# Planning layer 0's first expert block into the routing stage of a two-layer adaLN kernel

## The chip, the cores and the metric

The kernel runs on one core of a Trainium2 chip. The metric is device time in microseconds (us), the median of several runs. Engines: PE (TensorE, matrix multiply), DVE (VectorE), ACT (ScalarE), POOL (GpSimd, which here issues the indirect DMAs, that is, gathers and scatters by an index) and SP (SyncE, which issues plain DMAs).

## What is computed

Two layers on `x` of 4 x 1024 tokens with 256 features, everything in 32-bit floats. Each layer modulates normalised rows by a conditioning vector, adds a gated attention-like term, and then a gated mixture of experts. The change concerns layer 0's experts:

```python
h = _layernorm(x, axis=-1) * (1 + cb) + sb
x = x + gb * _L0_ffn_ref(h, ...)

# _L0_ffn_ref
logits = jnp.einsum('bsd,de->bse', input_emb, Wr) + br
route_w = jax.nn.softmax(logits, axis=-1)
_, topk_idx = jax.lax.top_k(route_w, TOP_K)          # 2 of 8 experts
...
h = jax.nn.relu(jnp.einsum('bsd,edh->ebsh', input_emb, W1) + b1[:, None, None, :])
expert_out = jnp.einsum('ebsh,ehd->ebsd', h, W2) + b2[:, None, None, :]
return jnp.einsum('bse,ebsd->bsd', routed, expert_out)
```

An expert maps 256 features to 1024 hidden units (W1) and back to 256 (W2).

## The kernel before

**Stage one** (to about 114 us) computes layer 0's attention term and the routing. Its work is a list of pieces given to a small planner, the class `Plan`: each piece has an engine, an estimated duration, the pieces it must follow, the buffers it holds, and a rank (lower goes first). `plan.run()` simulates the engines with these estimates and then emits the pieces in the order of their simulated start; on PE, ACT, DVE and POOL the instructions stand in exactly that order, and each engine executes its own list in order. The kernel's own estimates thus only set an order. SP's pieces are DMAs.

Normalised rows are stored into the DRAM table `h_rows` (one row of 256 features and two numbers, the "marks" `g_meta`, for each token), 512 KB at a time (L1318), and the marks by a second small DMA (L1305).

**Grouping tokens by expert.** Every token-expert pair is put into blocks of 128 pairs that share an expert. With counts of pairs by expert (`turn`, `total_staged`, `bases`), `close_staged` (a chain of small DVE operations, L598 to L651) works out which block belongs to which expert, `across` (PE, L690) spreads this over the partitions, `limits` (DVE) makes the limits of each block, and `list_weights` (DVE) the indices by which a block's weights are gathered. For one block j, `reach` (DVE, L754, tile `g_reached`), `look` (PE, L767, `pm_counts`) and `find` (DVE, L780 and L789) give the row numbers of its 128 tokens; `fetch` (POOL, L349, `xg`) gathers these rows. Block 0 is special: its limits come from `begin` alone, without `close_staged`. At the end of stage one, blocks 0, 1 and 2 are looked up. `kept_busy` puts matmuls of no use to the result on PE (`pm_busy`, L917).

**Stage two** runs the blocks in a loop written out by hand. Block j: transpose the gathered rows (`turn_rows`, PE, L1682, `pm_x`), copy them out of PSUM (`rows_turned`, DVE, L1687, `xT`), `hidden` (PE, L1729, `p_h`, 16 matmuls in two groups of eight), `rectified` (ACT, L1741, `hid`, bias and ReLU), `values` (PE, L1752, `p_y`, eight matmuls), `biased` (DVE, `y`), and a scatter of the result (POOL). In iteration j stand, in this order on PE: hidden(j), the transposes of block j+1, look-ups of later blocks, values(j-1). Weights lie in two buffers each for W1 and W2; `weights_in(j+1)` gathers W1 for the next block and does nothing where the expert is the one that the buffer already holds. The buffers of blocks 0 and 1 are loaded early in stage one by `first_weights` (SP), together with the gate `gb0` (128 x 1024 floats), which is first used after all of layer 0's early blocks.

The order around the change comes from the planner in stage one and from the loop in stage two. PSUM is shared out by three pools (`ps_1` and `ps_m` with three buffers, `ps_2` with two), handed out in turn: a piece that takes a buffer waits for the last reader of the one before it.

Of the kernel before, what the change touches and what calls it, by code (L numbers as in the profile page):

```python
# [19 lines left out]
P = 128  # L20
# [3 lines left out]
E = 8  # L24
# [117 lines left out]
def adaln_d2_kernel(  # L142
# [218 lines left out]
    class Pairs:  # L361
# [225 lines left out]
        def close_staged(self, scratch):  # L587


            J, blocks, runs, origin, up1 = self.J, self.blocks, self.runs, self.origin, self.up1  # L590
            begin2 = float(J - LATE)

# [10 lines left out]
            nc.vector.tensor_copy(blocks[:, :, 1:], blocks_i)  # L603
# [304 lines left out]

    plan = Plan(p1=3, p2=2, pm=3, xn1=5, h1T=2, xn2=6, h2T=2, t1=1, le=2)
# [301 lines left out]
    def second_half(b):  # L1211
# [73 lines left out]
        for gs in routed:  # L1285
            k, at = 4 * len(gs), 4 * gs[0] * B + b
            tag = (b, gs[0])

            def route(k=k, at=at, tag=tag):
                g0.route(pa, tiles["pl", tag[0], tag[1]][:, :, :E], br_sb, at, k, B)  # L1290

            d = plan(
                DVE,
                0.24 * 14 + 0.16 * 4 if k == NC else 0.22 * 14,
                route,
                after=[ready[g][0] for g in gs],
                holds=[ready[gs[-1]][1]],
                rank=rank - 0.2,
            )
            for g in gs:  # L1300
                of_batch["route", b, g] = d

            def mark(k=k, at=at):
                first = at - at % B
                nc.sync.dma_start(  # L1305
                    h_rows[first * P : (first + k * B) * P, D:].rearrange(
                        "(c b p) d -> b p c d", b=B, p=P
                    )[at % B],
                    g0.meta[:, at : at + (k - 1) * B + 1 : B, :],
                )  # L1310

            plan("SP", 1.0, mark, after=[d], rank=rank)
            for g in gs:
                back, slot, key = backs[g]

                def store(g=g, key=key):
                    at = 4 * g * B * P
                    nc.sync.dma_start(  # L1318
                        h_rows[at : at + 4 * B * P, :D].rearrange(
                            "(c b p) d -> b p c d", b=B, p=P  # L1320
                        )[b],
                        tiles["xn", key],
                    )

                plan("SP", 4.0, store, after=back, holds=[slot], rank=rank)
# [18 lines left out]
    def first_weights():  # L1344

        for i in range(2):
            nc.sync.dma_start(w1buf[i], W1[(E - 1) * P :, :])
            nc.sync.dma_start(w2buf[i], W2[(E - 1) * P :, :])
        gate_in(1, gb0)
# [26 lines left out]
    for piece in range(3):  # L1376
        ps = plan.slot("p2")
        m = loaded
        for k in range(KD):

            def mm(piece=piece, k=k):
                if k == 0:
                    tiles["rows1", piece] = psum(ps_2, [B, 2 * D], "pm_mod")
                nc.tensor.matmul(
                    tiles["rows1", piece],
                    lhsT=sT1[:, k, :B],
                    rhs=tiles["wm1"][:, k, 2 * D * piece : 2 * D * (piece + 1)],
                    start=(k == 0),
                    stop=(k == KD - 1),
                )  # L1390

            m = plan(PE, 0.87, mm, after=[m, of_batch["routed"]], holds=[ps], rank=20.0)

        def out_(piece=piece):
            modulation1(tiles["rows1", piece], piece)

        plan(ACT, 0.8, out_, after=[m], holds=[ps], rank=20.0)
# [9 lines left out]
    d = plan(DVE, 3.9, lambda: g0.close_staged(pa), after=[m], holds=[ps], rank=-1.0)  # L1407
# [9 lines left out]
    ps = plan.slot("p1")  # L1417
    m = plan(PE, 0.4, lambda: g0.across(ps_1), after=[d], holds=[ps], rank=-1.0)
    kept_busy(1.1, [m], 30.0)
    d = plan(DVE, 1.4, lambda: g0.limits(pa), after=[m, bs], holds=[ps], rank=-1.0)  # L1420
    plan(DVE, 1.2, lambda: g0.list_weights(pa), after=[d], holds=[ps], rank=-0.75)
    for j in range(AHEAD):
        ps = plan.slot("p1")
# [10 lines left out]
        first = -1.0 + 0.1 * j if j else -1.6  # L1434
        r = plan(DVE, 0.5, reach, after=[d] if j else [begun], rank=first)
        m = plan(PE, 0.25, look, after=[r], holds=[ps], rank=first)
        plan(DVE, 0.6, find, after=[m], holds=[ps], rank=first if j else -0.95)
        if j < AHEAD - 1:
            kept_busy(0.7, [m], 30.0 + j)
# [239 lines left out]
    def turn_rows(j):  # L1679
        pt = psum(ps_m, [P, KD, P], "pm_x")  # L1680
        for k in range(KD):
            nc.tensor.transpose(pt[:, k, :], xgbuf[j % 4][:, k:D:KD], ident)  # L1682
        return pt

    def rows_turned(pt):
        xT = work.tile([P, KD, P], F32, tag="xT", name="xT", bufs=3)
        nc.vector.tensor_copy(xT, pt)  # L1687
        return [xT[:, k, :] for k in range(KD)]

    def in_quads(j):  # L1690
        return 3 * QUAD <= j < turning

    def rows_of_block(j):
        if in_quads(j):
            return xgquad[j // QUAD % 2][:, j % QUAD, :]
        return xgbuf[j % 4]

    def quad_turned(j):

        rows = xgquad[j // QUAD % 2]  # L1700
        square = quads.tile([P, P // SQ, KD, QUAD, SQ], F32, tag="square", name="square", bufs=1)
        for k in range(KD):
            nc.vector.transpose(
                square[:, :, k, :, :].rearrange("p m b s -> p b m s"),
                rows[:, :, k:D:KD].rearrange("p b (m f) -> p b m f", f=SQ),
            )
        xT = quads.tile([P, P // SQ, KD, QUAD, SQ], F32, tag="xTq", name="xTq")
        for q in range(P // SQ):
            for m in range(P // SQ):
                nc.sync.dma_start(  # L1710
                    xT[m * SQ : (m + 1) * SQ, q, :, :, :], square[q * SQ : (q + 1) * SQ, m, :, :, :]
                )
        for b in range(QUAD):
            turned_quads[j + b] = [xT[:, :, k, b, :] for k in range(KD)]
            dests[j + b] = g0.aim(work, rows[:, b, :], j + b)

    def weights_in(j):
        gather(w1buf[j % 2], W1, g0.wrow[:, j : j + 1], E * P - 1)

    def weights_out(j):  # L1720
        gather(w2buf[j % 2], W2, g0.wrow[:, j : j + 1], E * P - 1)

    def hidden(j, xT, m4):
        w1 = w1buf[j % 2]
        p1 = psum(ps_1, [P, 4, P], "p1_h")
        for i in range(4):
            m = 4 * m4 + i
            for k in range(KD):
                nc.tensor.matmul(  # L1729
                    p1[:, i, :],  # L1730
                    lhsT=w1[:, k * H + m * P : k * H + (m + 1) * P],
                    rhs=xT[k],
                    start=(k == 0),
                    stop=(k == KD - 1),
                )
        return p1

    def rectified(j, hid, p1, m4):
        for i in range(4):
            m = 4 * m4 + i  # L1740
            nc.scalar.activation(  # L1741
                hid[:, m, :],
                p1[:, i, :],
                AF.Relu,
                bias=w1buf[j % 2][:, KD * H + m : KD * H + m + 1],
            )

    def values(j, hid):
        w2 = w2buf[j % 2]
        p2 = psum(ps_2, [P, D], "p2_y")  # L1750
        for m in range(KH):
            nc.tensor.matmul(  # L1752
                p2,
                lhsT=hid[:, m, :],
                rhs=w2[:, m * D : (m + 1) * D],
                start=(m == 0),
                stop=(m == KH - 1),
            )
        return p2

    def biased(j, p2):
        y = work.tile([P, D], F32, tag="y", name="y", bufs=3)
        nc.vector.tensor_tensor(y, p2, w2buf[j % 2][:, KH * D :], ALU.add)  # L1763
        return y

    dests, ys0, turned_quads = {}, {}, {}

    def aimed(j):
        dests[j] = g0.aim(work, xgbuf[j % 4], j)

    def kept(j):
        put("g0", dests[j], ys0[j])

    def new_hidden():
        return work.tile([P, KH, P], F32, tag="hid", name="hid")


# [18 lines left out]
    def once(j):  # L1796

        if j in (4, 5):
            gate_of(rows1[:, 3 * j - 10, :], rows1[:, 3 * j - 10, :], work)
        if j == 5:  # L1800
# [6 lines left out]
    with tc.manual_schedule(engines=ORDERED | {EngineType.SP}):  # L1807
        looks = {0: (3,), 1: (4,)} | {j: (j + 3, j + 10) for j in range(2, 9)}
        fetches = {j: (j + 2,) for j in range(4)} | {j: (j + 2, j + 8) for j in range(4, 10)}
        for j in range(2):  # L1810
            g0.fetch(rows_of_block(j), h_rows, j)
        xT, hid = rows_turned(turn_rows(0)), None
        aimed(0)
        for j in range(turning):
# [11 lines left out]
            new = new_hidden()  # L1826
            for m4 in range(2):
# [9 lines left out]
            if j:  # L1837
                ys0[j - 1] = biased(j - 1, values(j - 1, hid))
            if j % QUAD == 0 and in_quads(j + QUAD):
# [773 lines left out]
```

## Time and profile before

| what | us |
|---|---|
| median of 5 runs | 1112.48 (1110.62 to 1114.46) |
| the profiled execution's own time | 1113.93 |
| its span, first to last instruction | 1112.2 |
| PE busy | 1068.5 |
| DVE, ACT, POOL busy | 588.2, 429.4, 423.0 |

The span is cut into 40 equal slices of 27.8 us in the page; the change lies in the fourth and fifth (83 to 139 us). A line of the timeline has start, duration, engine, source line, operation, tile written `<-` tile read, and in square brackets the time the engine sat idle before it and what ended that. The chain of waits is the sequence of work that ended last, followed back from the end. In a table of windows, "PEclk" is the clock that TensorE was granted, 1.00 being full speed.

### The profile page before, as it was taken

The numbers are of one execution on the slowest core, as the hardware profiler recorded it, in microseconds if no ns is written. First come the engines' busy times: TensorE is split into PE (matmuls) and PEld (weight loads), VectorE is DVE, ScalarE is ACT, GpSimd is POOL, SyncE is SP. The second block draws the span as 40 slices with busy tenths as digits, with TensorE's granted clock in tenths as the row PEclk, the third lists the DMA queues.
The fourth block names the chain that finished last, engine by engine and source line by source line (L and its number), as shares of the span: only waits on it lengthen the run. The fifth ranks groups of instructions, "written<-read, shape, count | busy, mean of one in ns | idle before, by whom it ended". The sixth has DMA issues, their size and how long they took to land.

```text
span 1112.2 us, 18513 instructions
## 1 busy us (share of the span) xinstructions
PE 1068.5 (96%) x6142; PEld 837.4 (75%) x6142; DVE 588.2 (53%) x2284; ACT 429.4 (39%) x1164; POOL 423.0 (38%) x483
## 2 busy tenths in 40 slices
PE   7998999999999999999999999999999999999994
PEld 5895899998999999999989465665666577656751
DVE  7787343222222222221156488878588535698657
ACT  5977233322323233333344333423325325442531
POOL 2000566554555555554454010110116322743745
PEclk8999999999999999999999999999999999999998
DMA  9404423666552625343071211210004322441544
GB/s 317 187 21 115 155 89 111 246 202 206 166 177 57 211 59 170 103 139 123 20 256 40 73 57 48 62 34 19 1 25 137 96 72 81 128 131 60 170 113 149
DMA packets 86910, 128.69 MB, mean 116 GB/s; under 512 B 30412, under 2 KB 66517, under 8 KB 82206
## 3 DMA queue, kind: packets, MB, share of 16 engines
q0 software_dynamic: 31872, 69.68, 20.3%
q1 hardware_dynamic: 53838, 56.22, 15.9%
q10 hardware_dynamic: 1104, 1.58, 0.4%
q8 instruction: 51, 0.84, 0.3%
q14 instruction: 45, 0.37, 0.1%
HBM read 205.25 MB, written 30.22 MB: 212 GB/s over the span
## 4 chain that ended last, share of the span: by engine, by line
PE 80%; DVE 8%; DMA 7%; ACT 3%; issue 2%; POOL 0%; SPq 0%; DVEq 0%; ACTq 0%; POOLq 0%
PE p_h L1729 20%; PE p_u L2052 19%; PE p_y L1752 19%; PE p_f L2100 10%; PE p_e L2360 4%; DMA w<-in_W,g_wrow 3%; PE pm_x L2343 1%; PE pm_t L1664 1%; DMA xg<-gb_rows,gb_row 1%; ACT xn L1004 1%; PE pm_counts L767 1%; DVE ln_st L978 1%; PE pm_gram L1130 1%; PE pm_b L1071 1%; DMA yg<-y 1%
## 5 line engine op out<-in xcount | busy, mean ns | idle before, releaser
L1741 ACT ACTIVATE hid<-p_h,w 128x128 f32<-128x128 f32 x544 | 154.9, 368 | 317.2 <-issue 238.0
L1752 PE MATMUL p_y<-w,hid 128*128 128x256 f32 x1088 | 250.1, 383 | 3.2 <-DMA w<-in_W,g_wrow 3.2
L2052 PE MATMUL p_u<-hT,a 128*128 128x512 f32 x512 | 231.6, 596 | 1.6 <-ACTq L2015 0.8
L1752 PEld LDWEIGHTS p_y<-w,hid 128*128 128x128 f32 x1088 | 202.6, 191 | 28.6 <-DMA w<-in_W,g_wrow 3.6
L1729 PEld LDWEIGHTS p_h<-xTq,w 128*128 128x128 f32 x1536 | 179.1, 192 | 2.5
L1729 PE MATMUL p_h<-xTq,w 128*128 128x128 f32 x1536 | 179.2, 275 | 0.0
L2052 PEld LDWEIGHTS p_u<-hT,a 128*128 128x128 f32 x512 | 93.7, 190 | 98.3 <-issue 89.5
L349 POOL DMA_INDIRECT w<-in_W,g_wrow x134 | 135.2, 1009 | 76.8 <-ACT hid L1741 47.1
L1763 DVE TENSOR_TENSOR y<-p_y,w 128x256 f32<-128x256 f32 x68 | 28.8, 424 | 214.9 <-PE p_y L1752 195.1
L814 POOL DMA_INDIRECT y<-y,g_dest x68 | 69.6, 1024 | 136.8 <-DVE g_reached L754 66.9
L2100 PE MATMUL p_f<-a,hf 128*128 128x256 f32 x512 | 116.1, 380 | 0.0
L2100 PEld LDWEIGHTS p_f<-a,hf 128*128 128x128 f32 x512 | 96.1, 190 | 18.0 <-issue 5.9
L2148 POOL TENSOR_TENSOR x_sb<-x_sb,step 128x256 f32<-128x256 f32 x32 | 24.6, 769 | 207.6 <-DVE step L2141 153.7
L780 DVE TENSOR_SCALAR_CACHE_REDUCE g_hits<-pm_counts,g_nth 128x128 f16<-128x128 f32 x68 | 23.6, 347 | 104.3 <-PE pm_counts L767 104.2
L1729 PE MATMUL p_h<-xT,w 128*128 128x128 f32 x640 | 75.1, 276 | 2.1 <-DVE xT L1687 2.1
L1729 PEld LDWEIGHTS p_h<-xT,w 128*128 128x128 f32 x640 | 74.1, 192 | 3.3 <-DVE xT L1687 1.5
L2360 PE MATMUL p_e<-ew,xT 128*128 x280 | 71.2, 386 | 0.3 <-ACT y L2370 0.3
L2064 ACT ACTIVATE hf<-p_u,decay 128x512 f32<-128x512 f32 x56 | 38.2, 685 | 69.2 <-PE p_u L2052 67.1
L349 POOL DMA_INDIRECT xg<-h_rows,g_row x20 | 19.9, 996 | 105.6 <-DVE g_row L789 98.7
L349 POOL DMA_INDIRECT xg<-ga_rows,ga_row x39 | 37.3, 955 | 52.3 <-DVE g_hits L780 17.3
L2360 PEld LDWEIGHTS p_e<-ew,xT 128*128 128x128 f32 x280 | 49.1, 190 | 10.5 <-issue 3.9
L1622 DVE TENSOR_TENSOR h<-h,mod 128x256 f32<-128x256 f32 x128 | 51.5, 424 | 6.7 <-ACT h L1612 4.8
(376 smaller groups left out, 1333.0 us busy)
## 6 DMA issues: line engine op xcount, KB each, us to landing
yg<-y SPq DMA_DIRECT2D x32, 256.0 KB
xTq<-square SPq DMA_DIRECT2D x192, 32.0 KB
ga_y<-y SPq DMA_DIRECT2D x39, 128.0 KB
x_sb<-in_x SPq DMA_DIRECT2D x8, 512.0 KB
h_rows<-xn SPq DMA_DIRECT2D x8, 512.0 KB
gb_y<-y SPq DMA_DIRECT2D x31, 128.0 KB
out_x<-x_sb SPq DMA_DIRECT2D x7, 512.0 KB
a<-in_fw SPq DMA_DIRECT2D x6, 512.0 KB
```

Of the source, the lines that this page charges most:

```text
L349: return nc.gpsimd.indirect_dma_start(out=dst, out_offset=None, in_=table, in_offset=bass.IndirectOffsetOnAxis(ap=index, axis=0), bounds_c ...
L814: nc.gpsimd.indirect_dma_start(out=table, out_offset=bass.IndirectOffsetOnAxis(ap=dest, axis=0), in_=y, in_offset=None, bounds_check=2 * s ...
L1622: nc.vector.tensor_tensor(h, h, mods1[(sc, sh)[i]][:, b, :], (ALU.mult, ALU.add)[i])
L1729: nc.tensor.matmul(p1[:, i, :], lhsT=w1[:, k * H + m * P : k * H + (m + 1) * P], rhs=xT[k], start=(k == 0), stop=(k == KD - 1),)
L1741: nc.scalar.activation(hid[:, m, :], p1[:, i, :], AF.Relu, bias=w1buf[j % 2][:, KD * H + m : KD * H + m + 1],)
L1752: nc.tensor.matmul(p2, lhsT=hid[:, m, :], rhs=w2[:, m * D : (m + 1) * D], start=(m == 0), stop=(m == KH - 1),)
L1763: nc.vector.tensor_tensor(y, p2, w2buf[j % 2][:, KH * D :], ALU.add)
L2052: nc.tensor.matmul(pu, lhsT=a[:, k, m * P : (m + 1) * P], rhs=made["n1", c, "hT"][:, k, :, :], start=(k == 0), stop=(k == KD - 1),)
L2064: nc.scalar.activation(made[key, m], made[key, m, 0], AF.Silu, scale=decays[c])
L2100: nc.tensor.matmul(made[key, "p2", b], lhsT=made[key, m][:, b * P : (b + 1) * P], rhs=a1[:, m, :], start=(m == 0), stop=(m == KH - 1),)
L2148: nc.gpsimd.tensor_tensor(xs, xs, made[key, "step", b], ALU.add)
L2360: nc.tensor.matmul(made[key, "p2"], lhsT=made[key, "xT"][:, k, :], rhs=ew_flat[:, bass.ds(made[key, "at"] + k * D, D)], start=(k == 0), st ...
```

## The change

1. The first block of layer 0 moves into the planner's list (`first_block`): its gather, transposes, copy, hidden units in four pieces of four matmuls, ReLU, and the first four of its eight `values` matmuls. The other four are issued in iteration 0 of the loop; the loop's own hidden(0) and the gathers of blocks 0 and 1 ahead of the loop go. The order of PE in iteration 1 is then hidden(1), transposes of block 2, look 4, hidden(2).
2. Its operands lie in buffers not yet used: the hidden units in `gb0`, the transposed rows in `xgbuf[3]`. The copy out of PSUM is done by ACT rather than DVE. The load of `gb0` moves from `first_weights` to iteration 3 of the loop (SP).
3. `close_staged` is cut in two: `whole_blocks` (its first three instructions) stays ahead, the rest is planned after find 0. Look-ups 1 and 2 get later ranks, and block 1's gather stands on POOL behind `weights_in(1)`. The transposes of block 0 stand ahead of `across` on PE.
4. The gather of block 0 is planned after all stores into `h_rows` (`stores`), whose estimates change from 4.0 and 1.0 to 0.4 and a lag. In the order that results, the last row store stands ahead of the last store of marks; stage one's order is otherwise the same up to the last routes.
5. One of the three modulation pieces of layer 1 (`pm_mod`) moves behind look 0.
6. The three last `kept_busy` pieces (estimates 1.1, 0.7 and 0.7 us) go.

The diff's core; helper functions that only move up in the file, with optional arguments for halves, are left out:

```diff
-            plan("SP", 1.0, mark, after=[d], rank=rank)
+            stores.append(plan("SP", 0.4, mark, after=[d], rank=rank, lag=1.5))
...
-                plan("SP", 4.0, store, after=back, holds=[slot], rank=rank)
+                stores.append(plan("SP", 0.4, store, after=back, holds=[slot], rank=rank, lag=3.2))
...
             nc.sync.dma_start(w2buf[i], W2[(E - 1) * P :, :])
-        gate_in(1, gb0)
...
+    modulation_rows(of_batch["routed"], (0, 1))
...
-    d = plan(DVE, 3.9, lambda: g0.close_staged(pa), after=[m], holds=[ps], rank=-1.0)
+    whole = plan(DVE, 0.45, lambda: g0.whole_blocks(pa), after=[m], holds=[ps], rank=-1.0)
...
-    m = plan(PE, 0.4, lambda: g0.across(ps_1), after=[d], holds=[ps], rank=-1.0)
-    kept_busy(1.1, [m], 30.0)
-    d = plan(DVE, 1.4, lambda: g0.limits(pa), after=[m, bs], holds=[ps], rank=-1.0)
-    plan(DVE, 1.2, lambda: g0.list_weights(pa), after=[d], holds=[ps], rank=-0.75)
...
+    def first_block(found):
+
+        kept0 = tiles["first"] = {
+            "hid": gb0.rearrange("p b d -> p (b d)").rearrange("p (m t) -> p m t", t=P),
+            "xT": xgbuf[3][:, :D].rearrange("p (k t) -> p k t", t=P),
+        }
+        rows = plan(
+            POOL, 1.0, lambda: g0.fetch(xgbuf[0], h_rows, 0), after=[found, *stores], rank=-1.6, lag=1.3
+        )
+        ps = plan.slot("pm")
...
+        m = plan(PE, 0.35, turn, after=[rows], holds=[ps], rank=-1.5)
+        h = plan(ACT, 0.45, lambda: nc.scalar.copy(kept0["xT"], kept0["pt"]), after=[m], holds=[ps], rank=-1.5)
+        done = []
+        for m4 in range(2):
+            ps = plan.slot("p1")
+            for part in range(2):
...
+                h = plan(
+                    PE, 0.9, mm, after=[h], holds=[ps], rank=-0.3 if m4 or part else -1.5
+                )
...
+            values(0, kept0["hid"], kept0["p2"], range(4))
+
+        plan(PE, 1.75, mm, after=done[:1], holds=[ps], rank=-0.2)
+
     for j in range(AHEAD):
+        if j == 1:
+            closed = plan(
+                DVE, 3.1, lambda: g0.close_staged(pa), after=[whole, found], rank=-1.0
+            )
+            ps = plan.slot("p1")
+            m = plan(PE, 0.4, lambda: g0.across(ps_1), after=[closed], holds=[ps], rank=-1.0)
+            d = plan(DVE, 1.4, lambda: g0.limits(pa), after=[m, bs], holds=[ps], rank=-1.0)
+            plan(DVE, 1.2, lambda: g0.list_weights(pa), after=[d], holds=[ps], rank=-0.75)
...
-        first = -1.0 + 0.1 * j if j else -1.6
+        first = -1.3 + 0.4 * j if j else -1.6
...
-        plan(DVE, 0.6, find, after=[m], holds=[ps], rank=first if j else -0.95)
-        if j < AHEAD - 1:
-            kept_busy(0.7, [m], 30.0 + j)
+        found = plan(DVE, 0.6, find, after=[m], holds=[ps], rank=first)
+        if j == 0:
+            first_block(found)
+        elif j == 1:
+            plan(
+                POOL,
+                1.0,
+                lambda: g0.fetch(xgbuf[1], h_rows, 1),
...
+        if j == 0:
+            modulation_rows(m, (2,))
...
+        if j == 3:
+            gate_in(1, gb0)
...
-        for j in range(2):
-            g0.fetch(rows_of_block(j), h_rows, j)
-        xT, hid = rows_turned(turn_rows(0)), None
+        xT, hid = None, None
...
-            new = new_hidden()
-            for m4 in range(2):
+            new = new_hidden() if j else None
+            for m4 in range(2 if j else 0):
                 rectified(j, new, hidden(j, xT, m4), m4)
...
-            if j:
+            if j == 1:
+                ys0[0] = biased(0, tiles["first"]["p2"])
+            elif j:
                 ys0[j - 1] = biased(j - 1, values(j - 1, hid))
+            if j == 0:
+                values(0, tiles["first"]["hid"], tiles["first"]["p2"], range(4, KH))
```

## The prediction

> **What bounds the kernel now.** The page first: PE is busy for nearly all of the span and the chain that ended last is PE for four fifths. What is left to win lies where PE waits, so the next view is the chain of waits around the change, 100 to 136 us, and the timeline of GpSimd in it.
>
> ```profile
> PE 1068.5 (96%) x6142; PEld 837.4 (75%) x6142; DVE 588.2 (53%) x2284; ACT 429.4 (39%) x1164; POOL 423.0 (38%) x483
> PE 80%; DVE 8%; DMA 7%; ACT 3%; issue 2%; POOL 0%; SPq 0%; DVEq 0%; ACTq 0%; POOLq 0%
> ```
>
> ```profile
> 110.84 1.12 POOL L349 DMA_INDIRECT xg<-h_rows,g_row  x1 [98.70 <-DVE g_row L789]
> 113.38 0.95 POOL L349 DMA_INDIRECT xg<-h_rows,g_row  x1 [1.41 <-DVE g_hits L780]
> 114.69 1.02 POOL L349 DMA_INDIRECT w<-in_W,g_wrow  x1 [0.36 <-DVE g_code L738]
> ...
> 120.61 1.04 POOL L349 DMA_INDIRECT w<-in_W,g_wrow  x1 [3.65 <-ACT hid L1741]
> ```
>
> ```profile
> 115.36 3.81 PE p_h L1729 x32
> 119.17 0.25 PE pm_x L1682 x2
> 119.41 0.02 issue
> 119.44 0.43 DVE xT L1687
> 119.87 0.04 issue
> 119.92 3.84 PE p_h L1729 x32
> 123.75 0.23 PE pm_x L1682 x2
> 123.99 0.12 PE pm_counts L767 x2
> 124.11 3.51 PE p_y L1752 x16
> 127.61 3.57 PE p_h L1729 x32
> 131.18 0.24 PE pm_x L1682 x2
> ```
>
> Read: the gather of block 0 starts at 110.84, hidden(0) at 115.36, hidden(2) at 127.61, and from there PE never waits for long: a block is 7.55 us of PE (127.61 to 135.16 in the same view). The order of instructions of both kernels is the same before the last routes and from look 4 on, so I compare one instant: the start of hidden(2), 127.61. What moves it moves the end by as much.
>
> **The change part by part.**
>
> *Fetch 0.* Find 0 stood behind the 3.1 us of close_staged on VectorE (row at 110.56). Now only the three instructions of whole_blocks stand ahead (106.29 to 106.95 in the timeline: 0.66). Total ends at 105.70; whole_blocks to 106.4; begin and reach 0 take 0.68 (105.70 to 106.38), so 107.1; look 0, no longer behind a modulation matmul, ends at 107.3; find 0 took 0.55, so the row is there at 107.9 and GpSimd, 0.28 after it as before, at 108.2. But the gather also waits for all stores into h_rows, which before were long done:
>
> ```profile
> 106.00:107.00 1.00, 1.00 1.13 145
> 107.00:107.50 0.50, 1.00 0.82 109
> 107.50:108.00 0.50, 1.00 0.44 96
> 108.00:108.50 0.50, 1.00 0.13 21
> 108.50:109.00 0.50, 1.00 0.00 0
> ```
>
> Columns: window, length, granted clock, DMA share, GB/s. The last bytes land at about 108.3, and 0.5 us passed between the last bytes of gather 0 (113.3) and the PE that waited for it (113.82): 108.8. In the new order the last row store precedes the last 4 KB of marks, and nothing shows that tail by itself; a mark store after a row store ended about 0.8 us after it near 59 and 91, which would give 107.5. I take 108.5, ends 108.2 and 108.8: 2.3 us earlier than 110.84.
>
> *Hidden(0).* Gather start to transpose took 2.98 (110.84 to 113.82): transposes at 111.5. PE start to the copy's start is 0.55 in later blocks; a ScalarE copy twice as wide takes 0.57, so 0.4 here; 0.05 to PE: hidden(0) at 112.5, against 115.36. ScalarE is idle then (its idle time before L1741 was 8.96 us), so the copy has cover.
>
> *Across and the look-ups.* PE takes across behind the transposes, which wait for the gather: close_staged, now behind find 0, ends at 111.0, across starts at 111.75 rather than 110.18. Queued behind on VectorE are limits, reach 1 and list_weights. Limits start 0.52 after across, at 112.25; limits 1.26, reach 1 0.42, list_weights 1.06: 115.0. Hidden(0)'s first half (half of 3.81) ends at 114.4, look 1 0.15 later; its second half needs the PSUM buffer of across, freed by list_weights, so it starts at 115.05, a new wait of 0.5, and ends at 116.95. Look 2 and half of values(0) (3.51/2 = 1.75) end at 118.85.
>
> *Fetch 1.* GpSimd has weights_in(1) ahead of it now. Its index is ready at 114.85: start 115.1, 1.02 long, 0.30 to the next, so fetch 1 starts at 116.4, not 113.38, and its transposes at 119.4: PE waits 0.5. Then 0.36 of transposes and look 3, 1.75 of values(0)'s second half (which covers the xT copy), 3.57 of hidden(1): 125.1. There the values between hidden(1) and hidden(2) are gone, so the transposes, 0.55, copy and handover stand bare: 1.0. Hidden(2) at 126.1: **1.5 us earlier**. PE's work is otherwise the same; ScalarE's activations are the same eight.
>
> *The fillers.* Three kept_busy stretches go (pm_busy at 107.76, 110.50 and 113.16: 0.82, 1.24 and 0.82 us). They were on no path: PE waited anyway. What they covered is the granted clock. New PE work from 107.0 is 0.3 of look 0 and 1.74 of modulation (four passes at 0.43), then nothing from 109.05 to 111.5.
>
> ```profile
> 14.00:17.42 3.42, 2.02 (x13) 1.00 1.12 318
> 17.42:20.83 3.41, 1.64 (x11) 1.00 1.15 368
> 20.83:24.24 3.41, 2.53 (x10) 0.50 0.89 343
> ...
> 109.58:112.99 3.41, 2.28 (x11) 1.00 0.11 22
> ...
> 263.18:266.59 3.41, 1.30 (x13) 1.00 0.97 341
> 266.59:270.00 3.41, 2.86 (x7) 0.50 0.20 60
> 270.00:273.42 3.42, 3.42 (x24) 1.00 0.00 0
> ```
>
> Columns: window, length, PE busy, clock, DMA share, GB/s. The clock fell at 20.83 and at 266.59, 72 times 3.413 us apart, each time after a window of that grid with under half of it busy (1.64, 1.30); 2.02 and 2.28 kept it. The new gap of 2.45 us gives a window with 1.0 to 1.7 busy in about three of four alignments. Then some 1.35 us of hidden(0)'s first half is lost, but 0.5 of it lies in the wait for PSUM; look 1, find 1 and fetch 1 slip by 0.6: hidden(2) at 126.7, a gain of 0.9. If two windows are cold, as from 20.83 to 27.65, another 1.7 goes. The Trainium skill (TensorE: Matmul & The Clock Gate, "Why this matters for your kernels") asks for no PE gap over about 3 us; by that rule 2.45 us keeps the clock and the gain is 1.5. The two rows speak against it here: the gap before 266.59 was 2.66 us.
>
> *Gate load and SP.* gb0's 512 KB leave 25.26, where nothing waits for them, and are issued once values(0) has read the hidden units kept in gb0 (121.5). Their use is at 568.5, so 440 us cover them, but they meet weights_in(2). That one waited for ScalarE's read of block 0 and now stands behind fetches 1 and 2 (116.4, 117.65): start 119.0, landed and seen 5.9 us later by 120.61 to 126.5, so 124.9. The gate load adds 1.3 us at the 400 GB/s of the weights near 124: 126.2. It just fits. The mod piece that moved behind look 0, the planner's smaller SP costs, and the swap of the last two stores cost nothing: ScalarE and SP are idle there.
>
> **Sum.** 0.9 to 1.5 us by the clock, 0.3 more or less by the store tail: I take 1.3. Of the profiled execution's own 1113.93 (span 1112.2 and 1.73 around it) that leaves 1112.6; that run was 1.45 above the median of the five, so against 1112.48 it is 1111.2.
>
> **Rivals.**
> *Faster by more:* the marks land early (fetch 0 at 108.2, 0.3 more), the clock holds (1.5), and the look-up stretch of the kernel before, whose windows have 2.2 to 2.4 busy and in other alignments about 1.7, was cold in its typical run (0.5 to 1). Sum 1.8 to 2.8, so 1110.1. For it: the five runs spread over 3.8 us. Against it: clock 1.00 there in this profile.
> *Stores hold fetch 0:* rows and marks queue one behind the other and land at 109.5: gain 0.3 to 0.5, 1112.1. Against it: 1.58 MB at the 330 GB/s seen until 103.5 would end at 106.
> *Slower:* the gate load starves weights_in(2). About 1.2 MB would remain of both at 122.3. At 400 GB/s nothing is lost; below 254 GB/s the whole gain is gone; below 174 it is over 2.2 us slower. At the 145 GB/s of the row for 106 to 107, hidden(2) comes at 131.2, and that idle time makes the clock fall again (1.7): 5.3 later, 1117.8. For it: the load fetches the same four rows once for each of 128 partitions, and no row shows it alone. Against it: near 25 to 34 the same load ran among weights at 300 to 440 GB/s.
>
> **Chances.** A measurement of this kernel tells about 0.2% (2.2 us) from no change. Forecast 0.52; its 0.6 to 1.8 lies within 0.2%, but medians of runs that spread so err by about 1 us, so 0.16 of it lands beyond. Faster rival 0.24; stores 0.06; gate load 0.18. Faster 0.16 + 0.24 = 0.40; same 0.36 + 0.06 = 0.42; slower 0.18. The forecast's own range is 1109.7 to 1112.7; for 8 in 10 it reaches to 1108.3 (the faster rival's far end, with that 1 us) and to 1115.0 (the gate load at about 170 GB/s).
>
> **What would show it.** Right: gather 0 at 108.2 to 108.8, released by a DMA or VectorE; hidden(0) at about 112.5; PE waiting briefly for PSUM near 115 and for gather 1 near 119.4; a 0.50 clock in a window that begins between 111 and 113.7; hidden(2) at 126.1 to 126.7; 7.55 us blocks after. Wrong: gather 0 after 109.5; hidden(2) released by the weights' DMA; a second cold window; or a gain that comes or goes only near 264, in the wait for weights.

## The result and the profile after

The changed kernel takes 1116.38 us (median of 31 runs, 1112.78 to 1121.91), the kernel before in the same comparison 1112.31 (52 runs, 1108.93 to 1118.21). The ratio is 1.004 with a 95% interval of 1.003 to 1.005: slower by about 4 us, where 1.3 us less was forecast. The profiled execution of the changed kernel took 1120.74 us (span 1119.0), 4.4 above its own median; that of before was 1.45 above. So the 6.8 us between the two spans are more than there is to explain, and places are compared first, totals by the ratios.

The page after, its busy times and its chain by engine:

```profile
PE 1070.2 (96%) x6131; PEld 840.1 (75%) x6131; DVE 588.1 (53%) x2283; ACT 430.4 (38%) x1165; POOL 423.8 (38%) x483
PE 80%; DVE 7%; DMA 6%; ACT 3%; issue 2%; POOL 0%; SPq 0%; ACTq 0%; DVEq 0%; POOLq 0%
```

Nothing in them moves: PE is 1.7 us busier, and the span is 6.8 us longer. The counts hold what the experiments came down to: 11 TensorE matmuls and 11 weight loads fewer.

GpSimd around the change (start, duration, engine, line, operation; in brackets the idle time before it and what ended it), and the chain of waits from the first gather to hidden(2):

```profile
110.42 1.13 POOL L349 DMA_INDIRECT xg<-h_rows,g_row  x1 [98.32 <-DVE g_own L636]
116.76 1.02 POOL L349 DMA_INDIRECT w<-in_W,g_wrow  x1 [5.22 <-DVE g_code L743]
118.09 0.96 POOL L349 DMA_INDIRECT xg<-h_rows,g_row  x1 [0.30 <-issue]
```

```profile
108.80 0.16 DVE g_row L794
...
110.42 2.86 DMA xg<-h_rows,g_row
113.28 0.04 issue
113.32 0.50 PE pm_x L1429 x2
...
120.86 0.52 PE pm_x L1429 x2
121.39 0.28 PE pm_counts L772 x2
121.67 1.78 PE p_y L1501 x8
123.45 3.57 PE p_h L1477 x32
127.02 0.25 PE pm_x L1429 x2
...
127.30 0.43 DVE xT L1434
...
127.77 3.84 PE p_h L1477 x32
```

The pieces stand in the predicted order. But the row of block 0 is ready at 108.96 (108.80 + 0.16) and its gather starts 1.46 us later, where 0.28 was taken from before. Stage one itself ended 1.09 us later in this execution (its second `pm_turn` starts at 105.10, in before at 104.01). A window at half clock (a "cold" window below) lies ahead of it, from 98.53 to 101.95, but a repeat of the kernel before had one there too and its `pm_turn` at 103.97, so the cause of this 1.09 is not shown. Times below are counted from that `pm_turn`. Hidden(2)'s first matmul comes 22.67 us behind it, in before 23.44: a lead of 0.77.

The lead does not last to 280 us. PE's waits from 190 to 300 us, before and then after (waited for, us in total, times, longest):

```profile
PE p_y L1752 <- DMA w<-in_W,g_wrow: 3.2, 2, 2.7
```

```profile
PE p_y L1501 <- DMA w<-in_W,g_wrow: 3.7, 2, 2.7
```

The same two waits for gathered weights, near 206 and 265 us, in a stretch where the DMA engines are busy for 0.9 to 1.0 of the time; the first grew by 0.5. Behind them the stretch from `pm_turn` to the block at 279 us is 175.3 us in before and 175.4 in after.

The largest single difference of the two profiles lies far from the change, from the block that starts at 552 us to the one at 590 us: 38.21 us before, 41.11 after. A cold window from 586.64 to 590.05 is part of that in this profile; the repeats of the changed kernel have none there and take 39.3 and 39.8. In this stretch layer 0's blocks end and SP first loads scattered results back (`yg<-y`). GpSimd there, of before:

```profile
569.33 1.01 POOL L349 DMA_INDIRECT w<-in_W,g_wrow  x1 [0.31 <-PE p_h L1729]
572.29 1.01 POOL L349 DMA_INDIRECT w<-in_W,g_wrow  x1 [1.94 <-ACT hid L1741]
```

and of after, ahead of it a line of the DMA queues that has none like it in before (packets, MB, share):

```profile
q8 instruction: 1, 0.02, 1.2%
```

```profile
570.46 1.02 POOL L349 DMA_INDIRECT w<-in_W,g_wrow  x1 [0.31 <-PE p_h L1477]
576.74 1.22 POOL L349 DMA_INDIRECT w<-in_W,g_wrow  x1 [5.26 <-ACT hid L1489]
```

The windows of the queues are 560 to 565 and 562 to 567 us, from about 8 to 13 us behind the block's start at 552.05 and 9 to 14 us behind that at 553.15; this start is called the checkpoint below. In after a packet of queue 8, "instruction", lies in it: 16,384 bytes, 0.96 us long, at 564.3, that is 11.2 us behind the checkpoint. In before it came at 3.5 us. All of SP's later loads, ScalarE's use of them and GpSimd's weights follow late: 5.26 us of idle GpSimd in place of 1.94.

### The profile page after: what moved, and what is told of

It is laid out like the page before. It is cut to its first block, busy times and chain, and to the rows that moved or that the text cites. A ratio compares the mean times of both kernels' runs of the same rounds, so it can differ in the third digit from the quotient of the medians.

```text
span 1119.0 us, 18490 instructions
## 1 busy us (share of the span) xinstructions
PE 1070.2 (96%) x6131; PEld 840.1 (75%) x6131; DVE 588.1 (53%) x2283; ACT 430.4 (38%) x1165; POOL 423.8 (38%) x483
## 4 chain that ended last, share of the span: by engine, by line
PE 80%; DVE 7%; DMA 6%; ACT 3%; issue 2%; POOL 0%; SPq 0%; ACTq 0%; DVEq 0%; POOLq 0%
PE p_h L1477 20%; PE p_u L2127 19%; PE p_y L1501 19%; PE p_f L2175 10%; PE p_e L2435 5%; DMA w<-in_W,g_wrow 3%; PE pm_x L2418 1%; DMA xg<-gb_rows,gb_row 1%; PE pm_t L1834 1%; PE pm_counts L772 1%; ACT xn L1010 1%; ACT h2T L1055 1%; DVE ln_st L984 1%; DMA xg<-h_rows,g_row 1%; PE pm_b L1077 1%
## 5 line engine op out<-in xcount | busy, mean ns | idle before, releaser
L1501 PE MATMUL p_y<-w,hid 128*128 128x256 f32 x1072 | 246.7, 384 | 3.7 <-DMA w<-in_W,g_wrow 3.7
L1501 PEld LDWEIGHTS p_y<-w,hid 128*128 128x128 f32 x1072 | 199.9, 191 | 28.8 <-DMA w<-in_W,g_wrow 4.0
```

The costliest lines, as they stand in the source:

```text
L1501: nc.tensor.matmul(p2, lhsT=hid[:, m, :], rhs=w2[:, m * D : (m + 1) * D], start=(m == 0), stop=(m == KH - 1),)
```

## The experiments

The kernel before stood at 1112 us in some comparisons and at 1133 to 1138 us in others, so what is given are ratios to the kernel before of the same comparison. The theories: **clock** (the gap behind stage one makes TensorE's clock fall), **gate** (the moved gate load holds weights), and, once the stretch at 552 us had been read, **code** (TensorE's code is itself loaded in pieces by the DMA engines; 22 instructions fewer shift where each piece falls).

**Both kernels once more** (no edit).

> The kernel before, once more, for a second profile of it and the mean granted clock of more of its executions. All theories expect about 1112.4 us. The clock theory (the changed kernel loses to cold windows of TensorE) expects mean clocks near 0.991 here, that is one or two windows of 3.41 us fewer at half clock than in the changed kernel, whose runs had 0.985 to 0.991. The theory that the loss lies in waits for DMAs expects the same mean clocks in both kernels.

> The changed kernel, once more, for a second profile. All theories expect about 1116.4 us. The clock theory: mean clock 0.988 or so, and cold windows at places that differ from the first profile (near 99, 269, 587, 1071 us there) but about as many. The DMA theory: the same waits for DMAs as in the first profile, near 207, 266, 565 and 1065 us, each longer than in the kernel before. In both the block stage starts early: hidden(2) within 1 us of 127.6.

Measured: 0.9997 (0.9983 to 1.0011) and 1.0033 (1.0017 to 1.005). The loss repeats. The mean granted clocks were 0.9866 and 0.9848: lower in the changed kernel, as the clock theory says, but in before not the 0.991 that was expected. The windows of the repeat of the changed kernel, on its own 3.413 us grid (window, length, PE busy, clock, DMA share, GB/s):

```profile
109.18:112.59 3.41, 0.61 (x4) 1.00 0.14 41
112.59:116.00 3.41, 3.19 (x16) 0.50 0.00 0
```

and in the first profile after, where the clock held although the window had only 1.41 busy:

```profile
108.77:112.19 3.42, 1.41 (x4) 1.00 0.01 2
112.19:115.60 3.41, 2.06 (x15) 1.00 0.13 39
```

With the cold window hidden(2) came 23.61 us behind `pm_turn`, without it 22.67; 0.23 of the 0.94 between them is the gather of block 0, which started at 5.55 and 5.32.

**The gap filled.**

```diff
+                    if piece == 2 and k == KD - 1:
+                        pb = psum(ps_m, [P, 4 * P], "pm_fill")
+                        for _ in range(11):
+                            nc.tensor.matmul(pb, lhsT=busy16[:, :P], rhs=busy16, start=True, stop=True)
```

> The changed kernel with eleven matmuls of no use (about 2.4 us) behind the last modulation matmul on PE, in the gap of 3.1 us that PE has before the transposes of block 0. Clock theory, local form (the fillers that were removed kept the clock in this stage): 1.5 to 3 us faster than the changed kernel, 1113.5 to 1115. If the loss lies elsewhere (DMA waits, or cold windows in other stages): 1116.4, within 0.7.

Measured: 0.9993 (0.9983 to 1.0002); hidden(2) at 21.94. The whole loss is gone, about 4.5 us beside the changed kernel of the same comparison, which is more than the 1.7 us that hidden(2) won. That excess was the first sign that the clock was not all. Of the 1.7 itself, 1.1 is a gather that happened to start early in this profile (4.41 behind `pm_turn`, against 5.55); the four later profiles of filled forms have hidden(2) at 22.92 to 23.35.

**The gate load back among the first weights**, with the hidden units in a tile of their own.

```diff
-            "hid": gb0.rearrange("p b d -> p (b d)").rearrange("p (m t) -> p m t", t=P),
+            "hid": hid0,
...
-        if j == 3:
-            gate_in(1, gb0)
```

> The changed kernel with block 0's hidden units in a buffer of their own and the gate's load back at its old place among the first weights. Gate theory (the 512 KB now loaded in the block stage collide with the weights' gathers): 2 to 4 us faster than the changed kernel, 1112.5 to 1114.5. All others: 1116.4, within 0.7.

Measured: 1.0023 (1.0008 to 1.0038), beside 1.0033 for the changed kernel: a loss stays with the load at its old place, so the gate load is not all of it. The two differ by 0.0010, about 1.1 us, which is inside the intervals (0.0015 and 0.0017 to either side), so how large a part it has is not settled.

**As many TensorE instructions as before, nothing filled.** In the profile the eleven take 0.42 us together, and TensorE still waits further on in the opening (1.76 us at 15.3), so they cost next to nothing.

```diff
+        for _ in range(tiny):
+            nc.tensor.matmul(pb[:, :4], lhsT=busy16[:, :P], rhs=busy16[:, :4], start=True, stop=True)
...
-    plan(PE, 6.5, lambda: busy(5.0), holds=[ps], at=0.5, rank=-5.0)
+    plan(PE, 6.5, lambda: busy(5.0, tiny=11), holds=[ps], at=0.5, rank=-5.0)
```

> The changed kernel with 11 matmuls of 4 columns (22 TensorE instructions) behind the opening fillers, where TensorE waits for the first loads: as many TensorE instructions as the kernel before, nothing else moved. Code theory: TensorE's code comes in pieces of 16 KB, and with 22 instructions fewer one piece was asked for 11.2 us behind the checkpoint at 552 us instead of 3.5 us, and held the last packet of the scatter of y that the first load of yg waits for by 1.3 us. It should be asked for near 3 us again, the stretch from 552 to 590 us should take 38.2 to 39.2 us instead of 39.8 to 41.1, and the ratio to before should fall from 1.0033 to about 1.0015. Clock theory alone: the stretch stays at 39.8 or more, the ratio at 1.003. The gap behind the first stage keeps its cold window by both.

Measured: 1.0003 (0.999 to 1.0016), lower than the 1.0015 expected. The piece is asked for 2.8 us behind the checkpoint, the first `yg` load goes out at 12.7 instead of 13.7 to 14.5, the stretch takes 39.21. The clock theory said 1.003 and falls as the whole of the story: this profile has two cold windows behind the gap, hidden(2) at 24.48, and the mean granted clock of its executions (0.9842, in before beside it 0.9872) is no higher than that of the changed kernel (0.9848, in before beside it 0.9866).

**The gap filled with fewer instructions**: two float32 matmuls.

```diff
-                        for _ in range(11):
-                            nc.tensor.matmul(pb, lhsT=busy16[:, :P], rhs=busy16, start=True, stop=True)
+                        for c in range(2):
+                            rows = x_sb[:, c, 0:2, :].rearrange("p b d -> p (b d)")
+                            nc.tensor.matmul(pb, lhsT=ident, rhs=rows, start=True, stop=True)
```

> The changed kernel with two float32 matmuls of 512 columns (about 2.2 us by 275 ns for 128 columns) where the filler experiment had 11 float16 ones: the gap is filled with few TensorE instructions. Clock theory: no cold window behind the first stage, hidden(2) 21.9 to 22.0 us behind the second turn. Code theory: the piece of code still comes late, and 552 to 590 us still takes 39.8 to 41.1 us. Both together: ratio about 1.001, between the filler's 0.9993 and 1.0033. Clock alone: 0.9993. Code alone: 1.003.

Measured: 0.9993 (0.998 to 1.0006). It did not separate the two: the profile has four matmul records for the two, the piece came 3.6 us behind the checkpoint as in before, and the stretch took 37.51. There is no cold window, but hidden(2) came at 23.35, not at 21.9 to 22.0: the gather started at 5.80. The expectation that few instructions would leave the piece late was wrong, and a later run shows why: 8 instructions are enough.

**The kernel before without its three pieces of useless matmuls**, and the same padded to the old count.

```diff
-    kept_busy(1.1, [m], 30.0)
...
-        if j < AHEAD - 1:
-            kept_busy(0.7, [m], 30.0 + j)
```

> The kernel before without its three pieces of useless matmuls (22 TensorE instructions): nothing else of the change. Code theory: the piece of code is asked for near 11 us behind the checkpoint, 552 to 590 us takes 39.8 us or more, and the ratio is 1.001 to 1.002 from that alone. Clock theory: a cold window in the look-ups behind the first stage, hidden(2) 1 to 2.4 us later than 23.4 us behind the second turn, and the ratio 1.001 to 1.002 from that. Both: 1.002 to 1.004.

> The kernel before without its three pieces of useless matmuls, with the 11 matmuls of 4 columns behind the opening fillers, so that TensorE has as many instructions as in the kernel before. Code theory: the stretch from 552 to 590 us takes 38.2 to 39.2 us as in the kernel before. Clock theory: the look-ups behind the first stage have the same cold window as without the padding, ratio 1.001 to 1.002; if the pieces did nothing for the clock the ratio is 1.000.

Measured: 1.0037 (1.0024 to 1.005) and 1.0029 (1.0016 to 1.0041). Without padding the piece came at 11.3 us and the first `yg` load at 14.23; with it, 3.1 and 12.72. So the shift follows the count of instructions in either kernel, but padding brings only 0.0008 here, inside the intervals, where it brings 0.0030 to the changed kernel: the same shift of the piece, without a shown loss of the same size. At the old count the useless matmuls of before are worth 0.0029, some 3.3 us: without them the look-ups had two and three cold windows in a row, and hidden(2) came at 25.3 and 25.9.

**The forms side by side.**

> The changed kernel once more, on the chip of its padded and filled forms, so that the three can be compared in one call. Ratio to before 1.003 to 1.004 as so far.

> The changed kernel with 22 short TensorE instructions behind the opening fillers, once more. Code theory: the piece of TensorE's code comes near 3 us behind the checkpoint at 552 us, and the kernel is 1.5 to 3.5 us faster than the changed one of the same call. Clock theory alone: equal to the changed one.

> The changed kernel with the 11 useless matmuls in the gap (22 TensorE instructions), once more. What it gains over the padded form is the clock's share, since both have the same number of TensorE instructions: 0.5 to 2.5 us by the local times of hidden(2) (21.94 against 24.48 us behind the second turn), 0 if the weight waits near 206 and 264 us take the lead back.

> The changed kernel with two float32 matmuls in the gap, once more: like the filler, ratio to before 0.999 to 1.000; below 1.000 with the whole interval if it beats the kernel before.

Measured: changed 1.0044 (1.0019 to 1.0068), padded 1.0000 (0.9981 to 1.002), filled 0.9994 (0.9979 to 1.0009), filled in float32 1.0004 (0.9986 to 1.0022). In medians 1141.58, 1137.84, 1137.28 and 1137.63 us: the padding takes 3.7 us, the filling 0.6 more, which the intervals do not tell from nothing. Part of the 3.7 can be the clock's: the mean granted clock was 0.9812 changed and 0.9836 padded, and over the executions of these two forms and of before beside them a fit gives 0.5 to 0.9 us for each 0.001 of it, so 1.3 to 2.2 us by this estimate. In the first pair above the clock was not higher with the padding, and the loss went all the same. SP's wait ahead of the first `yg` load, of the changed and then of the padded kernel:

```profile
SPq L1699 <- DMA y<-y,g_dest: 9.9, 1, 9.9
```

```profile
SPq L1703 <- DMA y<-y,g_dest: 8.2, 1, 8.2
```

It waits for the same scatter, 1.7 us longer. But in this pair the stretch to 590 us took 39.27 changed and 39.77 padded: one profile does not carry the total.

**Other counts** (`tiny` 4, 22, 44 and 64).

> The changed kernel with 8 TensorE instructions more in the opening (4 matmuls of 4 columns). Theory of one place: if the piece of code is asked for near 3.6 us behind the checkpoint at 552 us, as with the two float32 matmuls, the ratio to before is 0.999 to 1.001; if it still comes near 11 us, 1.003 to 1.004. Theory of the count in general: about a third of the way, 1.002.

> The changed kernel with 44 TensorE instructions more in the opening. Theory of one place: the piece comes some 2 us ahead of where 22 put it (near 1 us behind the checkpoint), the scatter is not held, ratio 0.999 to 1.001. Count in general: another value, on either side.

> The changed kernel with 88 TensorE instructions more in the opening. Theory of one place: the piece comes 5 to 7 us ahead of where 22 put it, before the checkpoint, where the scatter ahead may be held but no load waits for it: ratio 0.999 to 1.001. Count in general: another value, on either side.

> The changed kernel with 128 TensorE instructions more in the opening, half a piece of code (256 instructions of 64 bytes in 16 KB). Theory of one place: the piece comes near 8 to 10 us ahead of the checkpoint, and the next one near 15 us behind it: ratio 0.999 to 1.001. If a ratio of 1.003 shows, another piece holds something in its turn.

| instructions added | piece, us from the checkpoint | first `yg` load | ratio |
|---|---|---|---|
| 0 (three profiles) | 11.1 to 11.2 | 13.7 to 14.5 | 1.0033 to 1.0044 |
| 8 | 3.4 | 12.41 | 1.0005 (0.9987 to 1.0023) |
| 22 (two profiles) | 2.8, 3.1 | 12.71, 12.29 | 1.0003, 1.0000 |
| 44 | 1.4 | 12.46 | 1.0009 (0.9996 to 1.0023) |
| 88 | -1.3 | 12.59 | 0.9999 (0.9986 to 1.0013) |
| 128 | -4.4 | 12.23 | 1.0015 (1.0004 to 1.0027) |

A step between 0 and 8, not a slope: in the ratio the theory of one place holds for 8 to 88. The pieces of 88 and 128 came later than expected (5 to 7 us ahead of the place with 22, and 8 to 10 ahead of the checkpoint). At 128 the loss is small and its cause was not found (the mean clock was the lowest of the four, 0.9879 against 0.9891 to 0.9898).

**The filled kernel and the kernel before at equal code**, both at 88 more than the changed kernel, where the profile had shown a wait of only 0.46 us for weights near 264 us.

> The changed kernel with the 11 useless matmuls in the gap and 66 short TensorE instructions in the opening: 88 more than the changed kernel. If the lead at hidden(2) (21.9 us behind the second turn) lasts once no piece of code holds the weights near 264 us: 1.5 us less than the form padded by 88, ratio 0.998 to 0.999. If the weight waits take it: 0.9995 to 1.000.

> The kernel before with 66 short TensorE instructions in the opening: as many as the form above. Its difference from the form above is the change with its gap filled, at equal code. If the wait of 2.66 us at 264 us in the kernel before is a piece of code's doing, it is 1 to 2 us faster than the kernel before, ratio 0.998 to 0.999; if not, 1.000.

Measured: 1.002 (1.0009 to 1.0032) and 1.0013 (1.0001 to 1.0025). Both expectations that this count is good fell: here it costs 1.5 to 2.3 us, and in the comparison before it cost nothing (0.9999), with the piece of code at the same place (-1.3, first `yg` load at 12.77); why is open. Between the two, 1136.21 and 1135.84 us: the replanning with its gap filled gives nothing that can be measured, with hidden(2) 0.46 us earlier (23.00 against 23.46).

No version beat the kernel before: the filled ones reach 0.9993 and 0.9994 with intervals that hold 1.000.

## Why the prediction was wrong

*Fetch 0.* This step failed first. Predicted was a gather 0.28 us behind the row or at the stores' landing, 108.5. The row came on time (108.96, against 107.9 and stage one's 1.09); the gather slipped by 0.8, and it was the stores that held it. The bytes had stopped by then, as the DMA share shows (window, length, PE busy, clock, DMA share, GB/s):

```profile
106.00:107.00 1.00, 0.80 (x7) 1.00 0.73 92
107.00:107.50 0.50, 0.00 (x0) 1.00 0.02 0
```

But the trace's semaphore records show the last row store complete at 109.24 and the last marks at 109.43, GpSimd passing its waits for them at 109.27 and 109.46, and the gather 0.98 behind the last completion. The prediction took the end of the bytes (108.3) for the landing and allowed 0.2 us, at most 0.5, from there to the gather. In before, too, the bytes ended at 108.4 and the last store was complete at 109.76 only, 1.08 ahead of the gather, not "long done". No run moved the stores alone, but over the fifteen profiles of the changed kernel and its variants the completion varies from 3.43 to 5.45 us behind `pm_turn`, and the gather follows it by 0.90 to 0.98 in every one. The rival "Stores hold fetch 0", which had a chance of 0.06, describes this wait.

In us behind the second `pm_turn` (of the changed kernel without filling, padded or not, the gate load where the change put it, there are nine profiles: the second, fourth and fifth rows):

| profiles | last store complete | gather 0 starts | cold windows behind the gap | hidden(2) | hidden(2) behind the gather |
|---|---|---|---|---|---|
| before, its repeat, with 66 more | 5.76, 4.10, 5.91 | 6.84, 6.85, 6.84 | 0 | 23.44 to 23.47 | 16.6 |
| changed, first profile | 4.33 | 5.32 | 0 | 22.67 | 17.35 |
| filled, five | 3.43 to 4.82 | 4.41 to 5.80 | 0 | 21.94 to 23.35 | 17.44 to 17.55 |
| without filling, five | 3.52 to 4.73 | 4.51 to 5.72 | 1 | 22.31 to 24.40 | 17.80 to 18.68 |
| without filling, three | 4.68 to 5.45 | 5.67 to 6.43 | 2 | 24.48 to 25.12 | 18.69 to 19.01 |

*Hidden(0), across, fetch 1.* Counted from the gather, this part of the sum was right: 17.6 us (108.5 to 126.1) against 17.35 to 17.55 where the clock held. The wait for PSUM is 0.3 where the clock held, against 0.5, and too short to be listed where it fell. The rival in which the gate load starves weights_in(2) did not occur in the first profile: hidden(2) was released by the DVE copy of xT, and the gate load went out at 123.48 only. In one of the nine, the repeat of the padded form, hidden(2) did wait for gathered weights, 0.96 us where the others wait 0.40 for xT, with the gate load issued at 123.21; whether that load was the cause is not shown.

*The clock.* The gap was 3.14 us in the first profile and 2.30 to 4.32 in the nine, not 2.45, because the gather came later. Eight of the nine had a cold window behind it, three of them two. Counted from the gather, one window cost 0.7 us in the mean (0.3 to 1.2, with 0.56 taken off for the wait for weights above), against 0.6 in the sum, and two cost 1.3; the case of two, for which 1.7 more stood in the text, was given no weight in the sum. The mean of the nine is 23.9, in before 23.4 to 23.5: a lead of 0.9 to 1.5 was forecast, and on the average hidden(2) is 0.4 later. Of the 1.8 us between the forecast without a cold window (22.1 behind `pm_turn`) and this mean, 1.1 is the later gather (5.55 against 4.49) and 0.7 the rest, most of it the clock. The Trainium skill (TensorE: Matmul & The Clock Gate, "Why this matters for your kernels") asks for no gap over about 3 us. Seven of the nine agree with that (gaps of 3.29 to 4.32, clock lost); a gap of 2.30 lost it and one of 3.14 kept it.

*"What moves hidden(2) moves the end by as much."* This step failed too: the place of hidden(2) does not tell the end in either direction. The lead of 0.77 was gone at 279 us, and the padded kernel ended level with before although its hidden(2) was 1.0 later (24.48, 24.40). The profile with 128 added has the latest hidden(2) of the nine (25.12) and the block at 279 us early, at 173.6 behind `pm_turn`; before without its useless matmuls was 1.9 and 2.4 behind before at hidden(2) and 5 to 6 behind it at 279. In the stretch to 280 us PE waits for gathered weights; the prediction's own last sentence named the wait near 264 and gave it no case. From 279 to 552 us all twenty profiles take 272.7 to 273.1, so nothing of the loss lies there. Beside it: the order of instructions being the same from look 4 on does not make the rest of the kernel the same.

*The fillers.* "They were on no path." Taken out of before at equal code, they cost 0.0029, with two and three cold windows in their place. And, what no view of the prediction asked, they were 22 instructions of TensorE's stream; the prediction put that at nothing.

**What the runs showed in their place.** At equal code the change is worth nothing (1.0000 and 1.0003 padded): the replanning wins back what the missing fillers lose (1.0029 without it). In the changed kernel the loss of 3.4 to 3.7 us appears when 22 instructions go and vanishes when 8 or 22 are put back in the opening, some 550 us ahead of where the trace shows an effect. This does not hold as a rule: in the kernel before, the same 22 put back brought only 0.0008, and 88 more cost nothing in one comparison and 0.0013 to 0.0020 in the next. The effect shown: with the piece of code at 11 us behind the checkpoint, the first `yg` load went out at 13.7 to 14.5 us in all five profiles; with the piece elsewhere, at 12.2 to 12.8 in all fifteen. The stretch from 552 to 590 us took 39.9 against 38.6 in the mean (39.6 without the first profile after and its cold window there), and single profiles without the piece reach 40.2. So 1.0 to 1.3 us of some 3.5 are placed; where the rest is lost stays open. Candidates are the waits near 264 us (1.27, 0.71 and 0.46 us with 8, 44 and 88 added, none with 128, 2.66 and 2.69 in before and after), but before has the wait too, and single profiles differ by as much (1.54 and 1.78 in the repeats of the two).

## What to carry to other kernels

When a change removes or adds instructions on a long unrolled stream, compare it with a form padded to the same count before any part of the time is put down to what the change was for; here 8 short instructions ahead of a wait were enough. Where an instruction waits for a store, count from the store's completion in the semaphore records and not from its last bytes: in the first profile after 2.3 us lay between them, and 0.98 more to the gather. A lead is worth something only up to the next place where another resource ends the wait, so follow it there before it is carried to the end. Useless matmuls that nobody waits for have two effects, on the clock and on the code's length, and a test that takes them away must separate the two.

## What the hardware showed that was not expected

TensorE's code arrived in 51 pieces of 16,384 bytes (queue 8, 0.84 MB in all), 0.88 to 1.84 us each on a DMA engine in before and after, in among the data. When a piece is asked for depends on the count of instructions ahead of it, and not smoothly: with 8 to 22 instructions fewer the piece at the checkpoint came 7.7 to 8.4 us later, about one block (7.98 us there), and met the tail of a scatter. What held it for so long is not shown; PE itself never waits over 0.27 us there. By the trace's DMA records the last of the scatter's 32 packets of 4,096 bytes ended 11.4 to 11.9 us behind the checkpoint in the fifteen profiles without the piece there, and 12.7 to 12.9 us in the five with it; the longest packet took 0.44 us in each of these five and 0.16 in each of the others. The Trainium skill (Runtime: NRT & Kernel Launch, "Instruction fetch mechanics") states blocks of 16 KiB and calls the crossing of a boundary mostly hidden; the size agrees with the packets here, and where the piece met a waited-for transfer it was not hidden.

The granted clock depends on more than the busy share of one window: in the first profile after, 1.41 of 3.42 us busy kept it (from 108.77) and 1.91 lost it (from 95.12). The prediction's line at half of a window thus does not hold exactly: 1.91 is over it, 1.41 under it.
